# State-space groups of two batches with partitions of their own, and layer 1's experts from the first tick past layer 0's pieces

## The chip, the cores and the metric

The kernel runs on one core of one Trainium2 chip. The metric is the device time of one execution in microseconds (us): the median of several runs. The engines are called PE (TensorE; PEld is its weight load), DVE (VectorE), ACT (ScalarE), POOL (GpSimd) and SP (SyncE, which here issues DMAs). Each has an in-order queue of its own: an instruction that waits holds up all that stand behind it on its engine.

## What is computed

The input is x of shape 8 batches x 512 positions x 128 channels in float32. Two blocks follow one another; each normalises, applies a per-batch scale and shift, runs a mixer, and does the same again with a feed-forward part. Cut to what matters here:

```python
# layer 0: attention (16 heads of 8), then a mixture of 8 experts, the two best for each token, and a shared one
x = x + ga * attention(layernorm(x) * (1 + ca) + sa)
x = x + gb * moe(layernorm(x) * (1 + cb) + sb)
# layer 1: selective state space with 16 states
xc = depthwise_conv(h, conv_w) + conv_b            # along the 512 positions, 4 taps
delta, B_in, C = parts of (xc @ Win + b_in)        # 16 states each
dA = softplus(delta) * A;  A_bar = exp(dA)
B_bar = where(|A| < eps, 1 + dA/2 + dA*dA/6, (A_bar - 1) / A_safe) * B_in
h_t = A_bar_t * h_(t-1) + B_bar_t                  # a scan along the positions
x = x + ga * ((C * h) @ Wout + b_out)
# layer 1: feed-forward
x1 = h + silu(pointwise(depthwise_conv(h)))        # 3 taps
rw = softmax of the two best of (x1 @ router)      # weights of 8 experts
m = out_w @ sum over e of rw[e] * silu(expert_w[e] @ x1 + expert_b[e]) + out_b
x = x + gb * (r + ff(r)),  r = rmsnorm(x1 + m)
```

All 8 experts of layer 1 are computed for every token and weighted; the state-space scan treats each batch and state as one row.

## The kernel before, in words

The program has three stretches. The first, attention, is written out slot by slot and isn't touched. The second works off layer 0's experts: a list `work` of n = 62 pieces of 256 rows, 31 + 15 of them routed ones (they fetch rows and weights by DMA) and 12 + 4 that apply the shared expert. One pass of the loop at the end of the kernel is a **tick**: in tick i, PE turns the input of piece i + 2 (`pxt`, copied by DVE to `xt`), does the first layer of piece i (`ph`, with ACT's activation to `hid`) and the second layer of piece i - 1 (`pyb`, copied by ACT to `yb` or `sh`). After that come the steps of layer 1 that were set for this tick by hand: `when(t, do, ...)` appends a step to tick t, and steps of one tick come in the order in which they were set. From tick n = 62 on there are no pieces left, and a tick is only its steps. So ticks are an order, not a clock: each engine runs through its own queue as its waits allow.

Per batch the steps of layer 1 are, in this order:

- `gather` (POOL, eight indirect DMAs of `yg` per batch), `combine` (DVE: adds the two routed experts to `sh`, then to x), `two_stats`, `ssm_root`, `ssm_centre` (ACT makes `xh`), `ssm_channels` (PE turns it, `ptn`; ACT makes `hq`), `ssm_conv` (DVE makes `xc`, in two halves), `ssm_bias`.
- `ssm_project` (L1225): PE multiplies two batches' `xc` to `pj`, and ACT copies it to three tiles `dl`, `bi`, `ci`, whose rows are (batch, state): 32 rows for two batches.
- The **chain**, once per group of batches, on those tiles: `chain_1` (two operations on DVE, then Exp and Ln on ACT), `chain_2` (DVE, four operations on POOL to `da` and `ts`, then Exp on ACT to `ab`), `chain_3` (DVE: `bs`, in the buffer of `da`), `chain_4` (the scan to `u`, then `ci`). ACT's table has to be loaded anew when its function changes between the experts' GELU or SiLU and Exp or Ln. `out_weights` makes `wo` on POOL.
- The **lead-in** of a batch (`lead_in`): `ssm_out` (PE `py`, DVE adds to x), statistics, `ffn_centre`, `ffn_channels`, `ffn_pointwise` (L1327: PE `pw`; DVE and ACT make `sl`; POOL adds it to x1), `ffn_logits` (PE `pl`), `ffn_ranks` (two comparisons on DVE, and `rk_eq` on POOL), `ffn_chosen`, `ffn_tanh`, `ffn_gates`, `ffn_gates_out` (PE `pgt`, ACT `gt`, SP writes `g_rows`). `later(t, us)` turns a delay in us into ticks, at 4.0 us for a tick before n and 2.2 after.
- The **experts**: `expert_in` (PE `pe`, ACT `ye`), three ticks later `expert_gate` (DVE: t = ye * gb, and POOL adds the t of several experts), `expert_sum` (PE `r`). `ffn_spread` brings `gb` from `g_rows` by DMA, 512 KB each, with 5 buffers. `base[b]` is the tick of a batch's first expert: n + 5 + 8b, and 5 more for batches 6 and 7. Then `rms_*` and `ff_*`.

Before, the groups are (0,1,2,3), (4,5), (6,7), and all use the same rows, from 0 on, of single-buffered tiles. Group 0 is projected at ticks 44 and 49, its chain runs in ticks 50 to 54, its lead-ins start at ticks 55 to 58. The tile `sl` shares the two buffers of the tag `xc` with the convolution's output. The memory of the experts' tiles (`gb`, `t`, `ye`) is that of layer 0's weights and activations, so it is only taken at tick n.

Of the kernel before, what the change touches and what calls it, by code (L numbers as in the profile page):

```python
# [19 lines left out]
P = 128  # L20
# [48 lines left out]
def tile_adaln_two_blocks(  # L69
# [222 lines left out]
    with tc.tile_pool(name="at", bufs=2) as at, tc.tile_pool(name="sc", bufs=4, space=PSUM) as psc, tc.tile_pool(  # L292
# [597 lines left out]
        def when(t, do, *args):  # L890
            events.setdefault(t, []).append(lambda: do(*args))
# [296 lines left out]

        GROUPS = ((0, 1, 2, 3), (4, 5), (6, 7))

        def place_in_group(b):

            h = next(h for h, g in enumerate(GROUPS) if b in g)
            j = GROUPS[h].index(b)
            return h, slice(32 * (j // 2), 32 * (j // 2) + 32), j % 2


        def ssm_root(b):
# [25 lines left out]

        def ssm_project(h, s):  # L1225

            if s == 0:
                for name in ("dl", "bi", "ci"):
                    held[name] = lt([P, S], name)[0 : 16 * len(GROUPS[h]), :]
            ps = flat(bank("pj"))  # L1230
            for i in range(2):
                xc = held.pop(("xc", GROUPS[h][2 * s + i]))
                for k in range(3):
                    pin(
                        T.matmul(
                            ps[32 * k : 32 * k + 32, :],
                            lhsT=k1["wip"][:, k, i, :],
                            rhs=xc,
                            start=(i == 0),
                            stop=(i == 1),  # L1240
                        )
                    )
            for k, name in enumerate(("dl", "bi", "ci")):
                A.copy(held[name][32 * s : 32 * s + 32, :], ps[32 * k : 32 * k + 32, :])

        def chained(h, name, tag=None):
            held[name] = lt([P, S], name, tag=tag)[0 : 16 * len(GROUPS[h]), :]
            return held[name]

        def of_states(h, name, i=0):  # L1250
            return k1[name][0 : 16 * len(GROUPS[h]), i : i + 1]

        def chain_1(h, step):

            dl = held["dl"]
            if step == 0:
                V.tensor_scalar(dl, dl, of_states(h, "bias"), None, ALU.add)
                u = chained(h, "u")
                V.scalar_tensor_tensor(u, dl, -1.0, dl, ALU.mult, ALU.min)
            else:  # L1260
                u = held["u"]
                A.activation(u, u, AF.Exp)
                A.activation(u, u, AF.Ln, bias=ones[0 : 16 * len(GROUPS[h]), 0:1])

        def chain_2(h, step):
            dl, u = held["dl"], held["u"]
            if step == 0:
                V.scalar_tensor_tensor(dl, dl, 0.0, u, ALU.max, ALU.add)
                da = chained(h, "da")
                G.tensor_scalar(da, dl, of_states(h, "asm"), None, ALU.mult)  # L1270
                ts = chained(h, "ts")
                G.tensor_scalar(ts, da, 1.0 / 6.0, 0.5, ALU.mult, ALU.add)
                G.tensor_tensor(ts, ts, da, ALU.mult)
                G.tensor_scalar(ts, ts, 1.0, of_states(h, "small"), ALU.add, ALU.mult)
            else:
                A.activation(chained(h, "ab"), dl, AF.Exp, scale=of_states(h, "an"))

        def chain_3(h, step):
            if step == 0:
                bs = chained(h, "bs", "da")  # L1280
                V.tensor_scalar(bs, held["ab"], -1.0, of_states(h, "inva"), ALU.add, ALU.mult)
            else:
                bs = held["bs"]
                V.tensor_add(bs, bs, held["ts"])
                V.scalar_tensor_tensor(bs, held["bi"], of_states(h, "bias", 1), bs, ALU.add, ALU.mult)

        def chain_4(h):
            hh, ci = held["u"], held["ci"]
            V.tensor_tensor_scan(hh, held["ab"], held["bs"], 0.0, ALU.mult, ALU.add)
            V.scalar_tensor_tensor(ci, ci, of_states(h, "bias", 2), hh, ALU.add, ALU.mult)  # L1290
# [8 lines left out]
        def ssm_out(b):  # L1299

            _, r, _ = place_in_group(b)
            wo = held.pop(("wo", b))
            py = bank("py1")
            for c in range(NC4):
                pin(
                    T.matmul(
                        py[:, c, :], lhsT=held["ci"][r, c * P : (c + 1) * P], rhs=wo[r, :], start=True, stop=True
                    )
                )
            V.tensor_add(xs[b], xs[b], py)  # L1310
# [16 lines left out]
        def ffn_pointwise(b):  # L1327
# [4 lines left out]
            x1 = flat(lt([P, NC4, D], "x1", tag="sh", bufs=B))  # L1332
            sl = lt([P, S], "sl", tag="xc", bufs=2)
            if b in GROUPS[0]:

                th = lt([P, S], "th", tag="gt1", bufs=2)
                A.activation(th, pw, AF.Tanh, bias=k1["pwb2"], scale=0.5)
                V.tensor_scalar(sl, pw, k1["pwb"], 0.5, ALU.add, ALU.mult)
                V.scalar_tensor_tensor(sl, th, 1.0, sl, ALU.add, ALU.mult)
            else:  # L1340
                A.activation(sl, pw, AF.Silu, bias=k1["pwb"])
            G.tensor_tensor(x1, hq[:, 2 : S + 2], sl, ALU.add)
            x1s[b] = x1
# [224 lines left out]

        base = [n + 5 + NE * b + (5 if b > 5 else 0) for b in range(B)]
        for b in range(B):  # L1570
# [3 lines left out]
        for b in range(B):  # L1574
# [3 lines left out]
            for i in range(NE // 2):  # L1578
                when(max(t - 3 + 2 * i, n + 5), ffn_spread, b, i)
            when(t - 1, ffn_residual, b)  # L1580
            when(t + 5, ffn_bias, b)
# [20 lines left out]
        for b, ts in enumerate(  # L1602
# [4 lines left out]
                (43, 44, 45, 46, 47, 48, 50),  # L1607
                (46, 47, 48, 49, 50, 51, 52),
                (49, 50, 51, 52, 53, 54, 55),
            )  # L1610
# [9 lines left out]
            for i in range(2):  # L1620
                when(ts[5], ssm_conv, b, i)
            when(ts[6], ssm_bias, b)
        when(44, ssm_project, 0, 0)
        when(49, ssm_project, 0, 1)
        when(53, out_weights, 0)
        chain(0, 50, (0, 0, 1, 2, 3, 3, 4))
        for b in GROUPS[0]:
            lead_in(b, 55 + b)
        when(59, ssm_project, 1, 0)


# [134 lines left out]
```

## Time and profile before

| | us |
|---|---|
| median of 3 runs | 1101.12 (1100.58 to 1102.52) |
| the profiled execution's own time | 1077.77 |
| its span, first to last instruction | 1075.8 |
| mean granted PE clock in it | 0.968 |
| PE, DVE, ACT, POOL busy | 1017.4, 671.2, 640.2, 485.7 |
| last matmul of layer 0's pieces ends | 854.7 |
| first `ye` of layer 1's experts starts | 865.9 |
| first t = ye * gb starts | 878.4 |

In the rows of the profile a group reads: start, duration (or busy time and mean), engine, line, operation, output <- inputs, shape, count, and in brackets how long the engine stood idle before it and what ended that. L65 is the helper that records nearly all operations of DVE, ACT and POOL, so these are told apart by their tiles. A matmul in float32 makes two records. The last quarter of the span, from about 740 us, is where layer 1's steps lie; tick 44 starts at 748.8, tick 54 at 802.3, tick 60 at 836.2, by the rows of `ph`.

### The profile page before, as it was taken

To read this page: it belongs to the slowest core of one execution; us is meant where nothing else is said; L and a number is where in the kernel's file an instruction comes from. 1 tells how busy PE (TensorE), PEld (TensorE's weight loads), DVE (VectorE), ACT (ScalarE), POOL (GpSimd) and SP (SyncE) were. 2 spreads that over 40 slices of the span, in tenths; PEclk is the share of its full clock that TensorE was granted. 3 is DMA by queue.
4 is the path that set the end of the run, shared out by engine and by line. 5 is a ranking of instruction groups with operands and counts; after the bars stand their busy time and mean duration, and the time that the engine had idled before them with its cause. 6 is when DMAs were issued, how large, how long until landed. Compare 5 with 4: busy or idle time off the path is not lost.

```text
span 1075.8 us, 24284 instructions
## 1 busy us (share of the span) xinstructions
PE 1017.4 (95%) x9584; PEld 667.6 (62%) x9584; DVE 671.2 (62%) x1292; ACT 640.2 (60%) x1404; POOL 485.7 (45%) x763
## 2 busy tenths in 40 slices
PE   9999999999999999999999999999899957777988
PEld 8655555555555555555568899988788634444556
DVE  5567767687777768776822014236765469778663
ACT  1166667676666767766664555645585563575554
POOL 3301314264454726443464313278541484567661
PEclk9599999999999999999999999999999988898999
DMA  9970000000000000000025878723542042213051
GB/s 274 283 237 2 2 2 12 2 18 15 9 24 2 28 5 14 19 6 27 12 90 167 240 235 246 212 72 83 160 143 74 16 134 93 75 60 132 17 186 40
DMA packets 94129, 93.25 MB, mean 87 GB/s; under 512 B 7568, under 2 KB 72432, under 8 KB 94016
## 3 DMA queue, kind: packets, MB, share of 16 engines
q1 hardware_dynamic: 89744, 83.02, 25.7%
q0 software_dynamic: 4096, 8.40, 2.7%
q8 instruction: 75, 1.23, 0.5%
q10 hardware_dynamic: 176, 0.30, 0.1%
q14 instruction: 38, 0.31, 0.1%
HBM read 60.33 MB, written 31.35 MB: 85 GB/s over the span
## 4 chain that ended last, share of the span: by engine, by line
PE 79%; DVE 9%; POOL 4%; ACT 4%; issue 3%; DMA 1%; SPq 0%; DVEq 0%; POOLq 0%; ACTq 0%
PE ps L512 23%; PE av L533 12%; PE pyb L1023 9%; PE ph L1012 8%; PE pm L484 5%; PE pmt L500 2%; PE ppt L551 2%; PE pw L1331 2%; PE idle L416 2%; PE r L1420 1%; DVE t L65 1%; PE pqk L443 1%; PE prow L392 1%; DVE xc L65 1%; PE pe L1432 1%
## 5 line engine op out<-in xcount | busy, mean ns | idle before, releaser
L65 DVE TENSOR_REDUCE mpad<-pm 128x2 f32<-128x1024 f32 x256 | 310.6, 1219 | 126.8 <-PE pm L484 126.4
L65 ACT ACTIVATE es<-ps 128x512 f32<-128x512 f32 x512 | 275.3, 598 | 141.5 <-PE pm L484 117.1
L512 PE MATMUL ps<-qt,kt 32*128 32x512 f32 x1024 | 291.4, 630 | 1.4 <-ACT es L65 0.7
L484 PE MATMUL pm<-kt,qt 32*128 32x512 f32 x1024 | 279.8, 646 | 0.3 <-DVE mpad L65 0.3
L533 PEld LDWEIGHTS av<-es,vaug 128*32 128x32 f32 x4096 | 104.2, 110 | 94.0 <-ACT part L65 43.2
L533 PE MATMUL av<-es,vaug 128*32 128x128 f32 x4096 | 137.7, 276 | 0.0
L512 PEld LDWEIGHTS ps<-qt,kt 32*128 32x128 f32 x1024 | 94.3, 183 | 63.2 <-issue 30.9
L65 ACT ACTIVATE hid<-ph,bias 128x256 f32<-128x256 f32 x184 | 72.1, 476 | 58.7 <-PE ph L1012 58.5
L767 POOL DMA_INDIRECT x_rows<-tok,ux x64 | 65.1, 1018 | 70.4 <-DMA x_rows<-tok,ux 61.5
L1023 PEld LDWEIGHTS pyb<-w2b,hid 128*128 128x128 f32 x736 | 90.9, 194 | 5.1 <-ACT hid L65 2.4
L1023 PE MATMUL pyb<-w2b,hid 128*128 128x128 f32 x736 | 91.4, 278 | 2.0 <-ACT hid L65 2.0
L1012 PE MATMUL ph<-xt,w1b 128*128 128x256 f32 x368 | 89.0, 386 | 0.0
L484 PEld LDWEIGHTS pm<-kt,qt 32*128 32x128 f32 x1024 | 78.2, 186 | 10.9 <-ACT kf L65 5.4
L65 POOL TENSOR_SCALAR qt<-qf,mask,zero 128x512 f32<-128x512 f32 x31 | 24.0, 776 | 130.2 <-PE pm L484 103.3
L1043 POOL DMA_INDIRECT yg<-y_rows,yrows x64 | 64.6, 1010 | 36.4 <-issue 18.2
L1432 PE MATMUL pe<-x,l1w_sb 128*128 128x512 f32 x128 | 71.9, 676 | 5.1 <-ACT ye L65 5.1
L1012 PEld LDWEIGHTS ph<-xt,w1b 128*128 128x128 f32 x368 | 67.7, 194 | 7.5
L65 DVE COPY xt<-pxt 128x256 f32<-128x256 f32 x46 | 19.1, 419 | 77.2 <-PE pxt L937 77.2
L65 ACT ACTIVATE ye<-pe,pc 128x512 f32<-128x512 f32 x64 | 43.2, 683 | 38.5 <-PE pe L1432 31.7
L65 POOL TENSOR_TENSOR t<-t 128x512 f32<-128x512 f32 x34 | 47.8, 1408 | 22.9 <-DVE t L65 21.4
L65 DVE TENSOR_TENSOR t<-ye,gb 128x512 f32<-128x512 f32 x64 | 54.5, 874 | 2.3 <-POOL t L65 2.3
L1420 PE MATMUL r<-l1w_sb,t 128*128 128x128 f32 x240 | 35.6, 297 | 16.4 <-POOL t L65 13.0
(301 smaller groups left out, 1562.5 us busy)
## 6 DMA issues: line engine op xcount, KB each, us to landing
x_rows<-zeros SPq DMA_DIRECT2D x16, 1024.0 KB
gb<-g_rows SPq DMA_DIRECT2D x32, 512.0 KB
w1b<-in_w1t SPq DMA_DIRECT2D x46, 256.0 KB
w2b<-in_w2t SPq DMA_DIRECT2D x46, 256.0 KB
xg<-x_rows SPq DMA_DIRECT2D x46, 128.0 KB
y_rows<-yb SPq DMA_DIRECT2D x46, 128.0 KB
x<-in_x SPq DMA_DIRECT2D x8, 256.0 KB
h_chan<-hf SPq DMA_DIRECT2D x8, 256.0 KB
```

Source lines behind the costliest of these rows:

```text
L65: return lambda *args, **kwargs: self.pin(call(*args, **kwargs))
L416: pin(T.matmul(ps[:, 0, :], lhsT=ident, rhs=ident, start=True, stop=True))
L484: T.matmul(pm[:, i, :], lhsT=qt[r : r + 32, qc * P : (qc + 1) * P], rhs=kt[r : r + 32, :], start=True, stop=True,)
L500: pin(T.transpose(pt[:, c, :], mpads[g % 4][:, c, :], ident))
L512: T.matmul(ps, lhsT=kt[r : r + 32, kc * P : (kc + 1) * P], rhs=qt[r : r + 32, :], start=True, stop=True)
L533: T.matmul(ps[32 * j : 32 * j + 32, 0, :], lhsT=vaugs[b % 2][:, kc, 4 * j + m, :], rhs=es_of[4 * g + kc, j][:, q], start=(kc == 0), stop=( ...
L767: nc.gpsimd.indirect_dma_start(out=x_rows[h], out_offset=IndirectOffsetOnAxis(ap=chosen["ux", b][:, k, c : c + 1], axis=0), in_=half[h]["t ...
L1012: pin(T.matmul(ph[:, f, :], lhsT=it["w1"][:, f * P : (f + 1) * P], rhs=it["x"], start=True, stop=True))
L1023: T.matmul(py[:, c, :], lhsT=it["hid"][:, f, c * P : (c + 1) * P], rhs=it["w2"][:, f, :], start=(f == 0 and "shared" not in it), stop=(f = ...
L1043: nc.gpsimd.indirect_dma_start(out=gathered[b][:, k, c, :], out_offset=None, in_=y_rows[h], in_offset=IndirectOffsetOnAxis(ap=half[h]["yro ...
L1420: T.matmul(ffn[b]["r"][:, c, :], lhsT=x[:, c * P : (c + 1) * P], rhs=w, start=(start and c == 0), stop=stop, skip_group_check=True,)
L1432: pin(T.matmul(pe, lhsT=l1w_sb[:, 2 + e, :], rhs=x1s[b], start=True, stop=True))
```

## The change

What it does:

- The groups are (0,1), (2,3), (4,5), (6,7). Group h has rows 32h to 32h + 31 of seven tiles (`dl`, `bi`, `ci`, `u`, `da`, `ts`, `ab`) that are allocated once; `bs` is written over `da`. So there are four chains of 32 rows instead of one of 64 and two of 32.
- Group 0 is projected at tick 44, with its chain in ticks 45 to 49 and lead-ins at 50 and 51; group 1 at tick 50, chain in 51 to 55, lead-ins at 56 and 57. Group 2 is projected at tick 60 (59 before).
- For batches above 1 the two halves of `ssm_conv` are in two ticks. Batches 4 and 5 are combined at ticks 50 and 53 (46 and 49 before), and their later steps follow.
- The experts start at tick n instead of n + 5. Nearly all that follows is 5 ticks sooner; the chain of group 2 and the lead-ins of batches 4 and 5 are 4 ticks sooner. The gathers of batches 6 and 7 keep ticks n - 2 to n + 3.
- `ffn_pointwise` writes into x1 at once; the tile `sl` is gone.

```diff
-        GROUPS = ((0, 1, 2, 3), (4, 5), (6, 7))
+        GROUPS = ((0, 1), (2, 3), (4, 5), (6, 7))
...
+            return b // 2, rows_of(b // 2), b % 2
+
+        def rows_of(h):
+            return slice(32 * h, 32 * h + 32)
...
+        def ssm_project(h):
+
+            if h == 0:
+                for name in ("dl", "bi", "ci", "u", "da", "ts", "ab"):
+                    k1[name] = lt([P, S], name)
             ps = flat(bank("pj"))
...
-                A.copy(held[name][32 * s : 32 * s + 32, :], ps[32 * k : 32 * k + 32, :])
+                A.copy(of(h, name), ps[32 * k : 32 * k + 32, :])
+
+        def of(h, name):
+            return k1[name][rows_of(h), :]
...
         def chain_3(h, step):
+            bs = of(h, "da")
             if step == 0:
-                bs = chained(h, "bs", "da")
-                V.tensor_scalar(bs, held["ab"], -1.0, of_states(h, "inva"), ALU.add, ALU.mult)
+                V.tensor_scalar(bs, of(h, "ab"), -1.0, of_states(h, "inva"), ALU.add, ALU.mult)
...
-            sl = lt([P, S], "sl", tag="xc", bufs=2)
-            if b in GROUPS[0]:
+            if b < 4:
 
                 th = lt([P, S], "th", tag="gt1", bufs=2)
                 A.activation(th, pw, AF.Tanh, bias=k1["pwb2"], scale=0.5)
-                V.tensor_scalar(sl, pw, k1["pwb"], 0.5, ALU.add, ALU.mult)
-                V.scalar_tensor_tensor(sl, th, 1.0, sl, ALU.add, ALU.mult)
+                V.tensor_scalar(x1, pw, k1["pwb"], 0.5, ALU.add, ALU.mult)
+                V.scalar_tensor_tensor(x1, th, 1.0, x1, ALU.add, ALU.mult)
             else:
-                A.activation(sl, pw, AF.Silu, bias=k1["pwb"])
-            G.tensor_tensor(x1, hq[:, 2 : S + 2], sl, ALU.add)
+                A.activation(x1, pw, AF.Silu, bias=k1["pwb"])
+            G.tensor_tensor(x1, hq[:, 2 : S + 2], x1, ALU.add)
...
-        base = [n + 5 + NE * b + (5 if b > 5 else 0) for b in range(B)]
+        base = [n + NE * b + (5 if b > 5 else 0) for b in range(B)]
...
-                when(max(t - 3 + 2 * i, n + 5), ffn_spread, b, i)
-            when(t - 1, ffn_residual, b)
+                when(max(t - 3 + 2 * i, n), ffn_spread, b, i)
+            when(max(t - 1, n), ffn_residual, b)
...
-                (46, 47, 48, 49, 50, 51, 52),
-                (49, 50, 51, 52, 53, 54, 55),
+                (50, 51, 52, 53, 54, 55, 57),
+                (53, 54, 55, 56, 57, 58, 60),
...
-                when(ts[5], ssm_conv, b, i)
+                when(ts[5] + (i if b > 1 else 0), ssm_conv, b, i)
...
-        when(44, ssm_project, 0, 0)
-        when(49, ssm_project, 0, 1)
-        when(53, out_weights, 0)
-        chain(0, 50, (0, 0, 1, 2, 3, 3, 4))
-        for b in GROUPS[0]:
-            lead_in(b, 55 + b)
-        when(59, ssm_project, 1, 0)
+        for h, t, lags in ((0, 44, (0, 1, 1, 2, 3, 4, 4)), (1, 50, (0, 0, 1, 2, 3, 3, 4))):
+            when(t, ssm_project, h)
+            when(t + 2, out_weights, h)
+            chain(h, t + 1, lags)
+            for b in GROUPS[h]:
+                lead_in(b, t + 6 + b % 2)
+        when(60, ssm_project, 2)
...
-        when(n + 8, out_weights, 1)
-        chain(1, n + 5, (0, 1, 2, 4, 6, 7, 8))
-        lead_in(4, n + 14)
-        lead_in(5, n + 18)
-        for b, t in ((6, n + 10), (7, n + 13)):
+        when(n + 3, out_weights, 2)
+        chain(2, n + 1, (0, 1, 2, 4, 6, 7, 8))
+        lead_in(4, n + 10)
+        lead_in(5, n + 14)
+        for b, t in ((6, n + 5), (7, n + 8)):
...
-        when(n + 20, out_weights, 2)
-        when(n + 27, ssm_project, 2, 0)
-        chain(2, n + 28, (0, 1, 2, 4, 6, 7, 8))
-        lead_in(6, n + 37)
-        lead_in(7, n + 44)
+        when(n + 15, out_weights, 3)
+        when(n + 22, ssm_project, 3)
+        chain(3, n + 23, (0, 1, 2, 4, 6, 7, 8))
+        lead_in(6, n + 32)
+        lead_in(7, n + 39)
```

More of the change, by code (lines that the diff above doesn't have):

```diff
@@ L1186, in channels @@
             return hq
-        GROUPS = ((0, 1, 2, 3), (4, 5), (6, 7))
+        GROUPS = ((0, 1), (2, 3), (4, 5), (6, 7))
         def place_in_group(b):
-            h = next(h for h, g in enumerate(GROUPS) if b in g)
-            j = GROUPS[h].index(b)
-            return h, slice(32 * (j // 2), 32 * (j // 2) + 32), j % 2
+            return b // 2, rows_of(b // 2), b % 2
+        def rows_of(h):
+            return slice(32 * h, 32 * h + 32)
         def ssm_root(b):
@@ L1223, in ssm_conv @@
                 held.pop(("hp", b))
[L1225 to L1229, printed above, removed]
+        def ssm_project(h):
+            if h == 0:
+                for name in ("dl", "bi", "ci", "u", "da", "ts", "ab"):
+                    k1[name] = lt([P, S], name)
             ps = flat(bank("pj"))
-            for i in range(2):
-                xc = held.pop(("xc", GROUPS[h][2 * s + i]))
+            for i, b in enumerate(GROUPS[h]):
+                xc = held.pop(("xc", b))
                 for k in range(3):
@@ L1243, in ssm_project @@
             for k, name in enumerate(("dl", "bi", "ci")):
-                A.copy(held[name][32 * s : 32 * s + 32, :], ps[32 * k : 32 * k + 32, :])
-        def chained(h, name, tag=None):
-            held[name] = lt([P, S], name, tag=tag)[0 : 16 * len(GROUPS[h]), :]
-            return held[name]
+                A.copy(of(h, name), ps[32 * k : 32 * k + 32, :])
+        def of(h, name):
+            return k1[name][rows_of(h), :]
         def of_states(h, name, i=0):
-            return k1[name][0 : 16 * len(GROUPS[h]), i : i + 1]
+            return k1[name][rows_of(h), i : i + 1]
         def chain_1(h, step):
-            dl = held["dl"]
+            dl, u = of(h, "dl"), of(h, "u")
             if step == 0:
                 V.tensor_scalar(dl, dl, of_states(h, "bias"), None, ALU.add)
-                u = chained(h, "u")
                 V.scalar_tensor_tensor(u, dl, -1.0, dl, ALU.mult, ALU.min)
             else:
-                u = held["u"]
                 A.activation(u, u, AF.Exp)
-                A.activation(u, u, AF.Ln, bias=ones[0 : 16 * len(GROUPS[h]), 0:1])
+                A.activation(u, u, AF.Ln, bias=ones[rows_of(h), 0:1])
         def chain_2(h, step):
-            dl, u = held["dl"], held["u"]
+            dl, u, da, ts = (of(h, name) for name in ("dl", "u", "da", "ts"))
             if step == 0:
                 V.scalar_tensor_tensor(dl, dl, 0.0, u, ALU.max, ALU.add)
-                da = chained(h, "da")
                 G.tensor_scalar(da, dl, of_states(h, "asm"), None, ALU.mult)
-                ts = chained(h, "ts")
                 G.tensor_scalar(ts, da, 1.0 / 6.0, 0.5, ALU.mult, ALU.add)
@@ L1275, in chain_2 @@
             else:
-                A.activation(chained(h, "ab"), dl, AF.Exp, scale=of_states(h, "an"))
+                A.activation(of(h, "ab"), dl, AF.Exp, scale=of_states(h, "an"))
         def chain_3(h, step):
+            bs = of(h, "da")
             if step == 0:
-                bs = chained(h, "bs", "da")
-                V.tensor_scalar(bs, held["ab"], -1.0, of_states(h, "inva"), ALU.add, ALU.mult)
-            else:
-                bs = held["bs"]
-                V.tensor_add(bs, bs, held["ts"])
-                V.scalar_tensor_tensor(bs, held["bi"], of_states(h, "bias", 1), bs, ALU.add, ALU.mult)
+                V.tensor_scalar(bs, of(h, "ab"), -1.0, of_states(h, "inva"), ALU.add, ALU.mult)
+            else:
+                V.tensor_add(bs, bs, of(h, "ts"))
+                V.scalar_tensor_tensor(bs, of(h, "bi"), of_states(h, "bias", 1), bs, ALU.add, ALU.mult)
         def chain_4(h):
-            hh, ci = held["u"], held["ci"]
-            V.tensor_tensor_scan(hh, held["ab"], held["bs"], 0.0, ALU.mult, ALU.add)
+            ci, hh = of(h, "ci"), of(h, "u")
+            V.tensor_tensor_scan(hh, of(h, "ab"), of(h, "da"), 0.0, ALU.mult, ALU.add)
             V.scalar_tensor_tensor(ci, ci, of_states(h, "bias", 2), hh, ALU.add, ALU.mult)
@@ L1306, in ssm_out @@
                     T.matmul(
-                        py[:, c, :], lhsT=held["ci"][r, c * P : (c + 1) * P], rhs=wo[r, :], start=True, stop=True
+                        py[:, c, :], lhsT=k1["ci"][r, c * P : (c + 1) * P], rhs=wo[r, :], start=True, stop=True
                     )
```

## The prediction

> **What bounds the kernel now.** I read the summary page first, then busy time by stretch, then the timelines of the engines around the seam between layer 0's expert pieces (ticks 0 to 62) and layer 1's experts (tick 62 on).
>
> ```profile
> PE 1017.4 (95%) x9584; PEld 667.6 (62%) x9584; DVE 671.2 (62%) x1292; ACT 640.2 (60%) x1404; POOL 485.7 (45%) x763
> ...
> PE   9999999999999999999999999999899957777988
> ```
> ```profile
> 748.80:808.00 59.20, 53.66 (x339) 46.25 (x338) 44.82 (x111) 41.62 (x90) 29.51 (x42) 0.94 0.52 150
> 808.00:854.70 46.70, 45.91 (x288) 36.00 (x287) 22.89 (x75) 25.96 (x61) 10.68 (x14) 1.00 0.17 47
> 854.70:878.40 23.70, 14.10 (x53) 7.01 (x51) 12.21 (x39) 10.99 (x17) 17.14 (x19) 0.86 0.41 127
> 878.40:925.00 46.60, 34.47 (x131) 19.83 (x131) 41.59 (x97) 24.91 (x51) 28.35 (x29) 0.89 0.28 91
> ```
>
> Columns: stretch, length, busy time of PE, PEld, DVE, ACT, POOL, then granted clock. Up to 854.7 TensorE is the bound (45.91 of 46.70). Then nothing is full for 23.7 us: the last piece is done at 854.7 and the first gated expert comes at 878.44. Behind it VectorE is nearly full (41.59 of 46.60). The seam is what the change works on. POOL, then DVE there:
>
> ```profile
> 867.22 0.94 POOL L1043 DMA_INDIRECT yg<-y_rows,yrows  x1 [0.30 <-issue]
> ...
> 875.61 0.73 POOL L65 TENSOR_TENSOR rk_eq<-rk_eq,tri 128x256 f32<-128x256 f32 x1
> 878.63 1.92 POOL L65 TENSOR_SCALAR da<-dl,asm 32x512 f32<-32x512 f32 x1 [2.29 <-DVE dl L65]
> ...
> 885.06 1.25 POOL L65 TENSOR_TENSOR t<-t 128x512 f32<-128x512 f32 x1
> ```
> ```profile
> 870.19 0.42 DVE L65 TENSOR_TENSOR rk_gt<-rk_gt,rk_eq 128x256 f32<-128x256 f32 x1 [5.85 <-POOL rk_eq L65]
> ...
> 878.44 0.67 DVE L65 TENSOR_TENSOR t<-ye,gb 128x512 f32<-128x512 f32 x1
> ...
> 883.63 4.19 DVE L65 TENSOR_SCALAR bs<-ab,inva 32x512 f32<-32x512 f32 x1
> ```
>
> VectorE waits 5.85 us for an rk_eq that stands in POOL's queue behind gathers, one each 1.25 us. So POOL's queue, with the rankings, sets the seam. The bs row is a state-chain step that took 4.19 us while POOL was busy beside it (1.58 in the chain before, at 801.62).
>
> Two more places:
>
> ```profile
> 769.43 1.48 PE L1184 MATMUL ptn<-ident,xh 128*128 128x128 f32 x4 [3.33 <-ACT xh L65]
> ...
> 770.97 3.42 PE L1012 MATMUL ph<-xt,w1b 128*128 128x256 f32 x8
> ...
> 793.94 3.60 PE L1023 MATMUL pyb<-w2b,hid 128*128 128x128 f32 x16 [2.04 <-ACT hid L65]
> 799.84 1.95 PE L1023 MATMUL pyb<-w2b,hid 128*128 128x128 f32 x16
> ```
> ```profile
> 788.14 1.28 ACT L65 ACT_TABLE_LOAD   x1
> 789.44 0.63 ACT L65 ACTIVATE u<-u 64x512 f32<-64x512 f32 x1
> ...
> 944.14 0.69 ACT L65 ACTIVATE sl<-pw,pwb 128x512 f32<-128x512 f32 x1 [4.87 <-PE pj L1235]
> ```
>
> **The change part by part.** Spans below are of the profiled execution: 1075.8 us between instructions, 1077.77 in all. The median of the runs shown is 1101.12, 23.35 more, which no row explains; I take gains off it unscaled.
>
> *One more chain in the pieces.* Groups of two batches make four chains, not three, and two stand before tick 62, not one. On ScalarE the program gains five table loads: 5 x 1.28 = 6.4, plus Exp, Ln, Exp at 0.63 + 0.72 + 0.72: 8.5 us. VectorE gains eight operations (0.45 + 0.68 + 0.67 + 1.58 + 0.68 + 0.74 + 1.21 + 0.74 = 6.8), POOL four (1.56 + 0.62 + 1.26 + 0.69 = 4.1). Half the partitions don't make them cheaper: bs, ts and ci have rows of the same length at 32 and at 64 partitions. VectorE has 14 of 59 us free there and hides it, POOL 30. ScalarE hides only part: its queue is in order, hid stands behind the loads, and TensorE waits for hid. The chain of before cost TensorE 2.04 waiting, 1.65 in the slow pyb (3.60 against 1.95) and some 0.6 in the two groups behind: 4.3. Two rules of the Trainium skill bear on this. ScalarE: Activation LUTs (What ACT_TABLE_LOAD costs) adds a drain of about 1.38 us to each load; the row has the next activation 0.02 us after the 1.28 load, so I take 6.4, where the rule would make 13.3, nearly 7 us more in front of hid and most of the gain gone. TensorE: Matmul & The Clock Gate (HAM oscillation) has the clock fall only after gaps above some 3.4 us; here gaps of 2.04 and 3.33 were both followed by slow matmuls. By the rule a chain costs 2.0, by the rows 4.3; I take 4.3.
>
> *The convolution split over two ticks.* At 763.39 the three longer convolution steps (4.79 us) kept xh of the next batch back: 3.33 waiting and about 2.6 in slow matmuls (ptn 1.48 against 0.60, ph 3.42 against 1.89, pyb 0.2). Now only the first half stands ahead of xh, so this 5.9 mostly goes; the first chain's Exp and Ln fall into the same tick and eat some of it.
>
> *Lead-ins sooner.* Rankings, tanh, gates and gates out of batches 0 and 1 move into the pieces, also batch 3's pointwise. Ahead of the gathers' place in tick 60 TensorE gets one pw (2.7), two pl (1.9), two pgt (1.2), a ptn (0.6), less a pj (1.9): +4.5, paid in full, since it is full there. Stalls between 748.8 and 854.7 were 6.2 waiting and 4.9 slow: 11.1. After: two chains at 4.3, less overlap with the old convolution stall, about 7.5 (bounds 4 and 15). So tick 60 comes 4.5 + 7.5 - 11.1 = 0.9 later (-3 to +8).
>
> *The seam.* Five ticks without experts go; all later work keeps its order, except that chain 2 and the lead-ins of 4 and 5 come one tick later beside the experts. The 16 gathers do not move: ticks 60 to 65, now with experts beside them and POOL's first t sum behind them. POOL from the first gather (847.28) to the end of the chain's ts (884.26) took 37.0. Now: 16 x 1.25 = 20, one x (1.1), two rk_eq (1.5), wo (0.85), four chain operations (5.35) = 28.8, and about 2.4 waiting for batch 3's pointwise: 31.2. That is 5.8 sooner, less 0.9. VectorE in turn waits at bs for POOL's ts (they share the da tile), and behind bs all gates are queued; but a combine pair (1.73) and a gate (0.68) that stood behind bs now stand ahead of it: +2.4. VectorE is the bound from there, so this carries on. Seam: 5.8 - 0.9 + 2.4 = 7.3. The spreads (SP, 0.33 each, 512 KB) are issued ticks sooner; SP is idle from 826 to 864, and their data wait for g_rows alone: nothing.
>
> *No sl tile.* sl shared two buffers with the convolution: at 944.14 ScalarE had waited 4.87 for a projection that comes later, with POOL's x and a t sum queued behind. Now the pointwise writes x1 itself. VectorE idled 2.26 and TensorE 1.75 after it: I take 2.7 (0 to 4.9).
>
> Sum: 7.3 + 2.7 = 10.0; 1101.1 - 10.0 = 1091.1, of the profiled kind 1067.8.
>
> **Rivals.**
> - *The whole seam goes.* If POOL's sums can lag (t has five buffers, and POOL idled 18 us between 885 and 925), the first gate sets the pace: about 8 us behind the pieces' end at some 856, 864 against 878.4: 14.4, plus 2.7: 17, 1084. For it: VectorE's own queue is short in ticks 62 to 65. Against: bs.
> - *The gathers swallow it.* POOL without a gap starves bs longer, tick 60 is 4 late, sl's wait was covered: 5.8 - 4 + 1 = 3, 1098. For it: the 4.19. That the row groups of one tile bind each other, so that the chains don't run free, would cost about as much.
> - *Slower: ScalarE in ticks 46 to 53.* Two chains, four xh and two projections' copies share that queue with hid. If three bursts each stall TensorE as xh did (5.9) and the convolution's stall stays, 23.6 replaces 11.1: tick 60 is 17 late, and 5.8 + 2.4 + 2.7 - 17 = -6: 1107. It decides once tick 60 is more than 10.9 late, that is with stalls over 17.5. For it: ScalarE is at 41.62 of 59.20 already. Against: the second pair of loads (799.5 to 802.8) stalled TensorE nowhere.
>
> **How the numbers follow.** Likeliest case (1086 to 1096) 0.46; whole seam (below 1086) 0.15; swallowed (1096 to 1101) 0.21; slower 0.18. Within 0.2% (2.2 us, about what a measurement of this kernel can tell from no change) are 1098.9 to 1103.3: part of the third case and a little of the last, 0.10; slower beyond 0.16; faster 0.74. The range leaves out the fastest tenth and the slowest tenth: 1083 to 1105.
>
> **What would show it.** Right: no xh stall of ptn at tick 47 to 48, pyb waiting twice for hid behind table loads, the first gather within 847 to 852, POOL's first t sum at 876 to 883 of the span, no wait of batch 5's pointwise for pj, the span near 1066. Wrong: TensorE idle over 10 us or a granted clock below 0.92 in ticks 44 to 60; the first t sum after 885; pxt copies late because VectorE is full in ticks 50 to 57.

## The result and the profile after

Side by side, the changed kernel took 1112.77 us (median of 4 runs, 1110.32 to 1118.78) and the kernel before 1100.85 (4 runs, 1099.77 to 1102.52): a ratio of 1.0115, 95% interval 1.0073 to 1.0157. It is slower by 1.15%; forecast was 1091.1. In that comparison both kernels carried some 23 us that no later comparison shows (last section), so the two are read below from a second comparison: 1088.11 beside 1078.16, ratio 1.0110 (1.0056 to 1.0165).

The summary page of the first profile of the changed kernel (own time 1110.32, span 1108.5), which answers to the one of before:

```profile
PE 1023.9 (92%) x9584; PEld 670.8 (61%) x9584; DVE 667.7 (60%) x1300; ACT 648.4 (58%) x1412; POOL 491.6 (44%) x767
...
PE   9999999999999999999999999869888965777988
```

TensorE does the same 9584 matmuls in 6.5 us more busy time. Its row has three slices of 8 on the way to the seam (the 6 and 5), where before had one; the 86 left of them, from 693 to 748 us, holds the 23 us, ahead of all that was changed.

The stretches of the second profile (own time 1086.70, span 1084.7), cut at the same events as before: tick 44; the point 1.8 us into tick 55; the end of the last piece; the first gated expert; then on to 925. Columns: stretch, length, busy time of PE, PEld, DVE, ACT, POOL, then granted clock.

```profile
749.90:823.90 74.00, 61.24 (x359) 49.61 (x358) 49.87 (x133) 52.71 (x104) 33.58 (x45) 0.92 0.44 125
823.90:871.70 47.80, 47.19 (x288) 36.60 (x287) 28.88 (x78) 24.76 (x60) 15.83 (x21) 0.99 0.31 95
871.70:879.60 7.90, 7.90 (x33) 4.56 (x32) 4.35 (x14) 7.01 (x9) 6.66 (x7) 1.00 0.13 34
879.60:925.00 45.40, 21.93 (x99) 14.07 (x98) 32.83 (x77) 17.49 (x32) 29.29 (x27) 0.74 0.25 79
```

The first stretch grew from 59.20 to 74.00, and TensorE, which was busy for all but 5.5 us of it, is now idle for 12.8 and at a granted clock of 0.92 (0.94 before). The second is as full as it was. The empty seam of 23.70 is now 7.90. But behind it TensorE does 21.93 in 45.40 where it did 34.47 in 46.60: the first experts come early and then stand still.

What TensorE waited for from 748 to 862, the view of waits, changed kernel; then the same of a repeat of the kernel before (span 1076.4). Columns: waiting line, releaser, total, times, longest.

```profile
PE pyb L1023 <- ACT hid L65: 6.5, 3, 3.5
PE py L1300 <- DVE ci L65: 3.4, 2, 2.9
PE pxt L937 <- ACT yb L65: 2.3, 1, 2.3
```
```profile
PE ptn L1184 <- ACT xh L65: 3.4, 1, 3.4
PE pyb L1023 <- ACT hid L65: 2.0, 1, 2.0
PE py L1306 <- DVE ci L65: 0.8, 1, 0.8
```

The wait for xh is gone, as meant. In its place hid is waited for three times (once before), yb once, and the wait for ci has grown from 0.8 to 3.4.

Profiled executions stand up to 8 us apart at tick 44 already (744.9 to 752.8), which the change does not reach. So I compare lengths from tick 44 on, by the rows of ph and pyb, one profiled execution each. The two of before differ by 0.9 in ticks 44 to 60, the two of the change by 1.7; a difference of 2 us or less between two rows shows little by itself.

| kernel | 44 to 50 | 50 to 55 | 55 to 60 | 44 to 60 | last piece's end to first t sum | last piece's end to the end |
|---|---|---|---|---|---|---|
| before, repeat | 34.2 | 23.9 | 30.3 | 88.3 | 30.3 | 221.4 |
| changed, repeat | 32.9 | 39.3 | 30.1 | 102.3 | 27.7 | 213.1 |
| before_conv_split | 32.8 | 23.1 | 29.4 | 85.3 | 30.3 | 220.9 |
| before_no_sl | 33.3 | 23.9 | 30.2 | 87.4 | 30.3 | 220.9 |
| before_gathers_last | 34.5 | 23.5 | 30.0 | 88.1 | 24.9 | 217.9 |
| before_no_tables | 35.1 | 19.5 | 30.7 | 85.3 | 30.3 | 218.5 |
| before_split_gathers_last | 33.3 | 22.3 | 29.4 | 85.0 | 24.1 | 217.0 |
| after_experts_late | 33.0 | 40.6 | 29.2 | 102.8 | 28.9 | 215.9 |
| after_gathers_last | 32.9 | 40.4 | 31.0 | 104.3 | 17.0 | 209.9 |
| after_no_tables | 26.9 | 39.8 | 29.2 | 95.9 | 27.9 | 213.3 |
| after_edges_on_dve | 31.4 | 37.5 | 29.9 | 98.8 | 27.8 | 213.1 |
| after_edges_no_tables | 25.5 | 37.9 | 29.1 | 92.5 | 27.8 | 213.0 |
| after_edges_lead_2_no_tables | 26.3 | 27.2 | 36.2 | 89.7 | 28.0 | 213.3 |
| after_edges_lead_1 | 34.1 | 29.9 | 33.1 | 97.1 | 27.3 | 213.4 |
| after_edges_lead_1_gathers_last | 32.3 | 29.3 | 35.2 | 96.9 | 16.1 | 206.7 |

The change loses 14.0 us between ticks 44 and 60, 1.0 more up to the last piece's end, and has 8.3 back by the end: 6.7 from tick 44 on, at the lower end of the 6 to 18 that the interval of the ratio gives. The loss lies in ticks 50 to 55.

### The profile page after: what moved, and what is told of

Its sections match the earlier page's. It is cut to its first block, busy times and chain, and to the rows that moved or that the text cites. A ratio compares the mean times of both kernels' runs of the same rounds, so it can differ in the third digit from the quotient of the medians.

```text
span 1108.5 us, 24293 instructions
## 1 busy us (share of the span) xinstructions
PE 1023.9 (92%) x9584; PEld 670.8 (61%) x9584; DVE 667.7 (60%) x1300; ACT 648.4 (58%) x1412; POOL 491.6 (44%) x767
## 4 chain that ended last, share of the span: by engine, by line
PE 74%; DVE 10%; POOL 6%; issue 5%; ACT 4%; DMA 1%; SPq 0%; POOLq 0%; DVEq 0%; ACTq 0%
PE ps L512 21%; PE av L533 11%; PE pyb L1023 8%; PE ph L1012 8%; PE pm L484 5%; PE pmt L500 2%; PE pw L1325 2%; PE ppt L551 2%; DVE t L65 1%; PE prow L392 1%; PE idle L416 1%; PE pqk L443 1%; PE r L1413 1%; DVE xc L65 1%; POOL yg L1043 1%
## 5 line engine op out<-in xcount | busy, mean ns | idle before, releaser
L1413 PE MATMUL r<-l1w_sb,t 128*128 128x128 f32 x240 | 35.2, 295 | 35.9 <-POOL t L65 33.6
L1425 PE MATMUL pe<-x,l1w_sb 128*128 128x512 f32 x128 | 66.8, 638 | 0.6 <-ACT ye L65 0.6
L1413 PEld LDWEIGHTS r<-l1w_sb,t 128*128 128x128 f32 x240 | 32.1, 205 | 46.3 <-POOL t L65 39.2
L65 ACT ACTIVATE ye<-pe,pc 128x512 f32<-128x512 f32 x64 | 43.1, 684 | 28.9 <-PE pe L1425 25.3
```

Source lines behind the costliest of these rows:

```text
L65: return lambda *args, **kwargs: self.pin(call(*args, **kwargs))
L1413: T.matmul(ffn[b]["r"][:, c, :], lhsT=x[:, c * P : (c + 1) * P], rhs=w, start=(start and c == 0), stop=stop, skip_group_check=True,)
L1425: pin(T.matmul(pe, lhsT=l1w_sb[:, 2 + e, :], rhs=x1s[b], start=True, stop=True))
```

## The experiments

Theory after the result: the pieces are late because of ScalarE's table loads for two chains. Rivals: the first chain's own way is too long for its ticks; the seam is what failed.

**Both kernels again.** No edit. First the kernel before:

> The kernel before, unchanged, for a second profile. In the profile of the changed kernel TensorE crawls from 711 to 737 us, one instruction each 2 us with no wait that the profile shows, and loses 22 us in a stretch that the change does not touch; the first profile of before has no such crawl, and its own execution (1077.77) lies 23 us under its median (1100.85). Theory: the crawl belongs to nearly every execution of both kernels and was missing in that one profile; then this execution takes 1098 to 1103 us, and its trace shows TensorE waiting 18 to 24 us between 700 and 745. Rival: the crawl is the changed kernel's own; then no crawl here, and if the time is near 1100 the 23 us lie elsewhere, spread over the span.

Measured 1078.24, with TensorE at full pace where the slow passage was expected: that theory fell, and the extra 23 us left the comparison. The next run's profile has no slow passage either, so they are not the changed kernel's own. Then the change:

> The changed kernel once more, beside the same runs of before as the others. The runs so far had before at 1077.3 us (no crawl of TensorE), and the kernel with the changed pieces but experts five ticks later at 1088.8. Theory: the five ticks bring little, since the first sum waits for the gathers either way: 1087 to 1091, a ratio to before of 1.009 to 1.013, as in the first comparison. Rival: the five ticks bring 8 to 10 us as the two profiles' tails suggest, and the 1.0115 came from the crawl: 1078 to 1081.

Measured 1088.11 beside 1078.16, ratio 1.0110. The loss is the change's own and has nothing to do with the 23 us.

**The convolution's halves in two ticks, alone.**

```diff
-                when(ts[5], ssm_conv, b, i)
+                when(ts[5] + (i if b > 1 else 0), ssm_conv, b, i)
```

> Before with one part of the change: the two halves of the convolution of batches 2 to 5 stand in two ticks. Theory: the wait of TensorE for xh at tick 48 (3.33 us, with 2.6 us of slow matmuls behind it) goes, and the rest stays: 4 to 6 us less than before, near 1096. Rival: the second half only moves into the next tick, where it delays the copies of the pieces' inputs, so that the stall moves along: within 1.5 us of before.

Measured 1074.69 (11 runs) beside 1077.26, ratio 0.9973 (0.9949 to 0.9996), 3.0 us in the stretch. This is less than the 4 to 6 that were expected: ptn still waits for xh, 2.42 us instead of 3.41. The trace shows what took the convolution's place: at 765.72 a step of 128x4 on VectorE, on the way to xh, takes 3.21 us while POOL works beside it; the same step took 0.16 in the kernel before.

**No sl tile, alone** (the last hunk of the change's `ffn_pointwise`, on the kernel before).

> Before with one part of the change: the pointwise writes x1 itself, and the tile sl, which shares two buffers with the convolution, is gone. Theory: ScalarE's wait of 4.87 us at batch 5's pointwise goes, and VectorE and GpSimd behind it gain 2 to 3 us: 1097.5 to 1099. Rival: TensorE had other work in those 5 us and VectorE is the bound there, so nothing is gained: within 1 us of 1100.9.

Measured 1078.98 (20 runs), ratio 1.0008 (0.9992 to 1.0023). ScalarE's 4.87 us wait is gone (the pointwise's activation waits 1.18), and the time does not move: that wait was covered.

**The change with its experts five ticks later again** (`base`, spreads, residual, chains 2 and 3 and lead-ins 4 to 7 shifted back).

> The changed kernel with its experts, and all that follows them, 5 ticks later again as in the kernel before; the four chains, the early lead-ins and the x1 without sl stay. Theory: the change loses about 15 us between ticks 44 and 61 and gets back 8 to 10 by the five ticks; then this kernel keeps the loss without the gain: 5 to 9 us above the changed one, 1118 to 1122. Rival: the five ticks bring nothing, since the first sum on GpSimd stands behind the same gathers either way (TensorE waits 20.4 us for it in the changed kernel): within 3 us of the changed kernel's 1112.8.

Measured 1088.76 (4 runs), ratio 1.0095 (1.0062 to 1.0128). The five ticks bring 2.8 us of the trace behind the pieces (215.9 to 213.1) and nothing that the runs can tell.

**Batch 7's gathers behind the first experts**, on each kernel:

```diff
-            when(n - 2 + k // 3, gather, PB[0] + k // 8, k % 8)
+            when(n - 2 + k // 3 if k < 8 else n + 4 + (k - 8) // 2, gather, PB[0] + k // 8, k % 8)
```

> The changed kernel with batch 7's eight gathers moved behind the first sums on GpSimd: two in each of ticks 66 to 69, not in ticks 62 to 65. Its combine at ticks 70 to 73 still finds them landed. Theory: GpSimd's queue of gathers sets the first sum (923.6 us in the changed kernel's profile, with TensorE idle 20.4 us before it): the sum comes 8 to 10 us sooner, and the kernel is 5 to 9 us faster than the changed one. Rival: VectorE's own queue with the chain's steps sets the pace of the experts: under 2 us.

> The kernel before with batch 7's gathers moved in the same way, to ticks 71 to 74 (two each). Theory: in the kernel before, too, the rankings and the first sum stand behind the gathers (VectorE waited 5.85 us for one): 3 to 6 us less than before, near 1073. Rival: the chain from logits to gates and spread sets the seam there: within 1.5 us of before.

On the change 1086.82, ratio 1.0107 (1.0051 to 1.0163): the first t sum comes 10.7 us nearer to the last piece, the end 3.2, and the runs show under 2. On before (n + 9) 1074.34, ratio 0.9980 (0.9964 to 0.9995). So the gathers hold the first sum, and the late pieces are a loss of their own.

**No table loads in the first two chains.** GELU takes the place of Exp, Ln and Exp there; the state space of batches 0 to 3 is not computed.

```diff
-                A.activation(u, u, AF.Exp)
-                A.activation(u, u, AF.Ln, bias=ones[rows_of(h), 0:1])
+                exp, ln = (AF.Exp, AF.Ln) if h > 1 else (AF.Gelu_apprx_tanh, AF.Gelu_apprx_tanh)
+                A.activation(u, u, exp)
+                A.activation(u, u, ln, bias=ones[rows_of(h), 0:1])
...
-                A.activation(of(h, "ab"), dl, AF.Exp, scale=of_states(h, "an"))
+                A.activation(of(h, "ab"), dl, AF.Exp if h > 1 else AF.Gelu_apprx_tanh, scale=of_states(h, "an"))
```

> The changed kernel with Exp, Ln and Exp in the chains of the first two groups replaced by the GELU that the pieces use, so that ten table loads of 1.28 us in ticks 44 to 55 go; this leaves out the true softplus and decay of batches 0 to 3. Theory: ScalarE's bursts of loads are the larger part of the loss in the pieces, two waits for hid of 2.27 and 2.45 with some 2.3 of slow matmuls behind each: 8 to 11 us faster than the changed kernel. Rival: the loss is VectorE's in ticks 49 to 57 and the moved work: under 4 us.

Measured 1079.29 (20 runs), ratio 1.0005 (0.9988 to 1.0023): 8.8 us faster than the change, 6.4 in the stretch. All waits for hid are gone, and the one for yb is 0.7 instead of 2.3. But one wait is longer:

```profile
788.83 2.04 PE L1301 MATMUL py<-wo,ci 32*128 32x128 f32 x8 [7.08 <-DVE ci L65]
790.80 3.63 PE L1235 MATMUL pj<-xc,wip 128*32 128x512 f32 x12
```

TensorE reached tick 50 sooner, and then waited 7.08 us instead of 2.92 for the first chain's last result, ci. Behind it pj took 3.63 us; it takes 1.92 in the kernel before. So a second delay lay beside the first. VectorE, then POOL, then TensorE of the change, repeat, show where it comes from:

```profile
779.71 3.98 DVE L65 TENSOR_SCALAR xc<-hq,pc 128x511 f32<-128x511 f32 x1 [4.13 <-POOL hq L65]
...
784.40 0.47 DVE L65 TENSOR_SCALAR da<-ab,inva 32x512 f32<-32x512 f32 x1
...
788.11 1.21 DVE L65 TENSOR_TENSOR_SCAN u<-ab,da 32x512 f32<-32x512 f32 x1
789.36 0.74 DVE L65 SCALAR_TENSOR_TENSOR ci<-ci,sbias,u 32x512 f32<-32x512 f32 x1
```
```profile
773.34 2.24 POOL L65 TENSOR_SCALAR da<-dl,asm 32x512 f32<-32x512 f32 x1 [5.33 <-DVE dl L65]
...
778.38 1.25 POOL L65 TENSOR_TENSOR x<-x,gab_rows 128x512 f32<-128x512 f32 x1
779.59 0.12 POOL L65 MEMSET hq<- 128x1 f32 x2
```
```profile
790.24 1.47 PE L1300 MATMUL py<-wo,ci 32*128 32x128 f32 x8 [2.92 <-DVE ci L65]
791.64 3.20 PE L1235 MATMUL pj<-xc,wip 128*32 128x512 f32 x12
```

Read it backwards. py waits for ci; ci stands on VectorE behind a convolution that waited 4.13 us; what it waited for is 0.12 us of POOL, the zeros at the edges of hq, and these stand in POOL's queue behind the first chain's four operations and an addition to x. Then the convolution took 3.98 us beside POOL's additions (0.54 when POOL was idle, in the kernel before). From here on the theory was that the zeros are the second delay.

**The edge columns written by VectorE**, alone and with the tables away:

```diff
-                G.memset(hq[:, 0:lead], 0.0)
+                (V if lead == 1 and b < 6 else G).memset(hq[:, 0:lead], 0.0)
```

(and the same for the tail's column.)

> The changed kernel with one thing moved: the zeros at the edge columns of hq (two columns of one element a row) are written by VectorE and not by POOL, for the convolution's hq of batches 0 to 5. In the trace of the changed kernel VectorE stands 4.13 us before the convolution of batch 3, for these two columns, which stand in POOL's queue behind the four operations of the first chain; the convolution then takes 3.98 us instead of 0.6 beside POOL's additions to x, and the first chain's scan stands behind it, and TensorE's py waits 2.92 us for that. Theory (a short POOL write on the way of the first chain is part of the loss): that wait of py goes, and the kernel is 3 to 5 us faster than the changed one: 1083 to 1085 beside a before of 1077 to 1078, a ratio near 1.006. Rival (only ScalarE's table loads bind): within 1.5 us of the changed kernel, ratio near 1.010.

> The kernel above, and besides the chains of the first two groups use GELU in place of Exp, Ln and Exp, so that ScalarE loads no table there; what is computed is no longer the state space of batches 0 to 3. With the tables alone away TensorE waited 7.08 us for the first chain's ci (2.92 with them), so the two delays lie beside each other. Theory (two delays of about equal length, tables and the chain's way through POOL and VectorE, either of which holds tick 50): with both away the kernel is 5 to 7 us faster than with the tables alone away (1079.3), so 1072 to 1074, a ratio near 0.995, and tick 60 comes no later than in the kernel before plus the 4.5 us of moved matmuls. Rival (what is left is simply TensorE's and VectorE's added work): within 2 us of 1079.

Alone 1084.93 (6 runs) beside 1076.19, ratio 1.0077 (1.0052 to 1.0102); 3.5 us in the stretch. That is the theory's number, but its interval overlaps that of the change, and the wait that was to go is there: py waits 2.85 us. With the tables away 1077.27 (14 runs), ratio 1.0001 (0.9983 to 1.0019): the rival's number. The trace has 3.4 us less in the stretch, of which the runs show next to nothing, and py still waits 5.91.

Why the wait stays, VectorE and then POOL show, edges alone:

```profile
773.63 1.53 DVE L65 TENSOR_SCALAR xc<-hq,pc 128x511 f32<-128x511 f32 x1 [0.79 <-ACT hq L65]
775.20 6.03 DVE L65 SCALAR_TENSOR_TENSOR xc<-hq,pc,xc 128x511 f32<-128x511 f32 x1
```
```profile
775.69 2.49 POOL L65 TENSOR_TENSOR x<-x,gab_rows 128x512 f32<-128x512 f32 x2
778.18 2.49 POOL L65 TENSOR_TENSOR x<-x,gab_rows 128x512 f32<-128x512 f32 x2
```

The convolution no longer waits 4.13 us for the zeros, but its next step takes 6.03 us and ends just after POOL's four additions to x; in the change, where it came behind them, that step took 0.75. With the tables away two such steps took 6.57. From dl to the end of ci the first chain needs 17.0 us with the edges on VectorE and 17.6 in the change. So the zeros alone did not hold it: once they are away, by the rows, the convolution beside POOL's additions does. Of the 3.5 us some 1.4 come sooner, at batch 2's convolution, whose zeros had stood behind gathers in POOL's queue (VectorE waited 3.13 us for them), and 1.6 because py and pj took 1.12 and 1.92 us this time. Moving the additions to another place was not tried, so that the wait for ci is theirs is argued and not shown.

**One chain's tables in the kernel before** (the same edit there; batches 0 to 3 again).

> The kernel before with GELU in place of Exp, Ln and Exp in the one chain that stands in layer 0's pieces; what is computed is no longer the state space of batches 0 to 3. It prices one chain's table loads in the old place. Theory (one chain's loads cost TensorE 4.3 us, as the prediction had it from a 2.04 wait and a slow group behind it): 1074, ratio 0.996; then the loads of two chains would be worth 8.6, which is what the changed kernel lost. Rival (in the old place the loads are mostly hidden, and it is the new place, beside the convolutions and projections of batches 2 and 3, that makes them dear): within 1.5 us of before.

Measured 1076.69 (14 runs), ratio 0.9997 (0.9981 to 1.0012). In the trace ticks 50 to 55 lose 4.4 us and the stretch 3.0; in the runs nothing. The profiled execution was 2.6 us late by tick 30 already, where nothing was edited. Behind the last piece it has 2.9 us less than before, where nothing was edited either. So single profiles differ by as much as this edit is worth in them.

**More ticks for the first chain.** Lead-ins of batches 0 and 1 later, by two ticks without tables, by one with them:

```diff
-                lead_in(b, t + 6 + b % 2)
+                lead_in(b, t + 6 + b % 2 + (2 if h == 0 else 0))
```

> The changed kernel with hq's edge columns written by VectorE, GELU in place of Exp, Ln and Exp in the chains of the first two groups (their state space is left out), and the lead-ins of batches 0 and 1 two ticks later (52 and 53), so that the first chain has seven ticks instead of five. With the same lead-ins as in the change this kernel took 1077.3, and TensorE waited 5.91 us for ci with slow matmuls behind it (pj 3.63 instead of 1.9, py 2.04 instead of 1.1), 8.7 in all. Theory (that one wait is the rest of the loss): the last piece ends 7 to 9 us sooner, near 856 of the span, and the kernel takes 1070 to 1072, a ratio near 0.994. Rival (TensorE's moved matmuls are the rest, and the wait only shows where slack lay): within 2 us of 1077, and TensorE idles elsewhere in ticks 50 to 58.

> The changed kernel with hq's edge columns written by VectorE, and the lead-ins of batches 0 and 1 one tick later (51 and 52); all is computed, and all tables are loaded. With the edges alone it took 1084.9, and py waited 2.85 us for ci. Theory (the first chain is too long for five ticks): that wait goes, with its slow matmuls 4 us: 1081, a ratio near 1.004. Rival (the tick that is freed is filled by hid behind the second chain's tables, which moves with nothing): within 1.5 us of 1084.9.

Without tables 1074.46 (22 runs) beside 1077.64, ratio 0.9972 (0.9953 to 0.9991), about 3 us better than without the two ticks; 2.8 in the stretch. That is between the two expectations. TensorE's waits there:

```profile
PE ptn L1184 <- ACT xh L65: 2.3, 1, 2.3
PE pj L1235 <- DVE xc L65: 1.5, 1, 1.5
```

The wait for ci is gone, but two others stand in its place. With the tables 1081.57 (11 runs), ratio 1.0043 (1.0019 to 1.0067): 0.34% better than with the edges alone, near the 4 us expected, of which the stretch shows 1.7. The wait for ci is gone here too, but the waits for hid rose from 6.2 to 8.4 us, which is the rival's mechanism at a smaller size.

**All three mended**: edges, one tick, and batch 7's gathers last.

> The kernel above, and batch 7's gathers in ticks 66 to 69 instead of 62 to 65, behind the first experts' sums on POOL. Theory (once the pieces are on time the seam is POOL's, and its first sum sets the rest): 3 to 5 us under the kernel above, 1077, about even with the kernel before. Rival (VectorE behind the first gate is the bound, as in the changed kernel, where the same move gave under 2): within 2 us of the kernel above.

Measured 1075.57 (22 runs) beside 1077.64, ratio 0.9973 (0.9959 to 0.9988). This has all of the change in it and beats the kernel before. Here the gathers' move is worth 6.7 us of the trace and 0.7% of the time, in the trace twice what it gave either other kernel; why, is not settled.

**The two small gains on the kernel before.**

> The kernel before with the two small gains joined: the convolution's halves of batches 2 to 5 in two ticks (alone ratio 0.9973), and batch 7's gathers in ticks 71 to 74 (alone 0.998). Theory (the first shortens the pieces, the second the seam, so they add): ratio 0.9953, 1072 to 1073. Rival (both end in the same first gate, where VectorE is the bound behind): no better than the convolution alone, 0.997 to 0.998.

Measured 1074.06 (22 runs) beside 1076.19, ratio 0.9980 (0.9966 to 0.9995): no better than either alone, though the trace of one execution adds them up (span 1070.0). Its interval overlaps that of the mended change; the runs do not tell which is the best.

## Why the prediction was wrong

**The step that failed: "stalls 11.1, after about 7.5, so tick 60 comes 0.9 later (−3 to +8)".** Tick 60 came 14.0 later, because the stalls did not fall to 7.5 but rose to some 21.7. Counted in the rows of ticks 44 to 60 as the prediction counted them, waiting and slow matmuls together:

| TensorE's stalls, us | before, repeat | change, repeat | in the prediction, after |
|---|---|---|---|
| behind ScalarE's chain work: hid, in the change yb too | 4.3 | 14.1 | 8.6 for two chains |
| for ci | 0.8 | 5.0 | absent |
| for xh | 5.9 | 0 | part of −1.1, with the rest |
| the rest | 0.5 | 2.6 | |
| sum | 11.5 | 21.7 | 7.5 |

The other part of the 14.0 is moved matmuls: 3.9, the foreseen 4.5 less a pgt that stands behind tick 60's ph.

The experiments took parts away one after the other. Each step but the last changes one thing, the first in both kernels; the runs are differences of medians or of ratios:

| step | us of ticks 44 to 60 | us in the runs | in the prediction |
|---|---|---|---|
| the change's tables (102.3 − 95.9), less those of before (88.3 − 85.3) | 3.4 | 8.8 less 0.3 | 4.3 for one more chain |
| edge columns off POOL's queue (95.9 − 92.5) | 3.4 | 0.4; with tables 3.6 | absent |
| two more ticks for the first chain (92.5 − 89.7) | 2.8 | 3.1 | absent |
| what is left against before without tables (89.7 − 85.3) | 4.4 | | −3.4: moved matmuls 4.5, the convolution −5.9, overlap and other stalls −2.0 |
| sum | 14.0 | | 0.9 |

The two tables answer different questions. The first says what TensorE waited for; the second says what came back when that was taken away. With the tables away nearly all of the 14.1 went, but the stalls for ci grew from 5.0 to 11.1 (7.5 of it waiting), so the trace gives back only 6.4. For the price of one more chain the traces say 3.4 and the runs some 8, and this stays open. By the runs the loss goes when the two chains' tables go (ratio 1.0110 with them, 1.0005 without), but with all tables loaded the edges and one more tick take more than half of it away too (1.0043). The parts overlap and do not add.

The slower rival, "decides with stalls over 17.5", put the stalls at 23.6, tick 60 at 17 late and the time at 1107. Its direction, its place and its cause, bursts on ScalarE that hold hid, were right by the rows: three such bursts of 6.0, 4.1 and 4.1 us are the 14.1. The convolution's stall, which it kept, went, and the wait for ci, which it had not, came.

Point by point:

- *A chain's price.* 4.3 each, read from the one chain of before, was too small for the new place: by the rows the first cost 6.0 behind hid and the second 8.2 behind hid and yb. "The second pair of loads stalled TensorE nowhere" held in the kernel before; in the change the second pair of each chain did. ScalarE of the change, repeat, with the second chain's first loads and its second pair, then TensorE:

```profile
804.24 1.28 ACT L65 ACT_TABLE_LOAD   x1
805.54 0.72 ACT L65 ACTIVATE u<-u,ones 32x512 f32<-32x512 f32 x1
806.27 1.28 ACT L65 ACT_TABLE_LOAD   x1
807.57 1.57 ACT L65 ACTIVATE hid<-ph,bias 128x256 f32<-128x256 f32 x4
...
816.39 1.28 ACT L65 ACT_TABLE_LOAD   x1
817.68 0.72 ACT L65 ACTIVATE ab<-dl,an 32x512 f32<-32x512 f32 x1
818.41 1.28 ACT L65 ACT_TABLE_LOAD   x1
819.70 1.57 ACT L65 ACTIVATE hid<-ph,bias 128x256 f32<-128x256 f32 x4
821.14 0.39 ACT L65 COPY yb<-pyb 128x256 f32<-128x256 f32 x1
```
```profile
808.10 3.58 PE L1023 MATMUL pyb<-w2b,hid 128*128 128x128 f32 x16 [2.46 <-ACT hid L65]
...
821.59 0.69 PE L937 MATMUL pxt<-ident,xg 128*128 128x128 f32 x2 [2.29 <-ACT yb L65]
```
```profile
808.10:811.50 3.40, 3.40 (x16) 3.40 (x17) 3.29 (x7) 3.40 (x10) 3.14 (x3) 0.52 0.13 39
```

  Each load is followed 0.02 us later by its activation; no row has the 1.38 us drain that the Trainium skill gives in ScalarE: Activation LUTs (What ACT_TABLE_LOAD costs). And 2.46 us of idling were followed by a group of 3.58 us instead of 1.95, at a granted clock of 0.52 (last row), though the Trainium skill, TensorE: Matmul & The Clock Gate (HAM oscillation), names only gaps above some 3.4 us. So the rows were the better guide to both. But a gap of this length does not always cost it: in the kernel with the edges on VectorE a wait of 2.85 us was followed by matmuls at a clock of 1.00 (787 to 791 us).
- *"VectorE and POOL hide it."* This is where the wait for ci comes from. By share of busy time both had room. By order they had not: with five ticks from projection to lead-in, the first chain's scan stood on VectorE behind a convolution that waited for POOL and then ran slowly beside POOL's additions. The prediction had seen such a row at the seam (bs, 4.19 us "while POOL was busy beside it") and did not look for it in the pieces. It costed each engine's work and never laid out the chain's way from dl to ci against the tick in which py asks for it.
- *The convolution.* "This 5.9 mostly goes": it went in the change, where ptn no longer waits. Done alone it gave 3.0. As a stall it was replaced: the kernel with two more ticks still has about as much stalling, 9.3, as before without tables, 8.8.
- *Moved matmuls.* 4.5 foreseen, 3.9 by the rows up to tick 60.
- *The seam and sl.* 7.3 + 2.7 = 10.0 foreseen, 8.3 came, but not as told. POOL from the first gather to the end of the chain's ts took 36.0 (863.36 to 899.34, the changed kernel's repeat), where 31.2 was foreseen and before had 37.0:

```profile
863.36 1.10 POOL L1043 DMA_INDIRECT yg<-y_rows,yrows  x1 [0.16 <-issue]
...
871.48 1.09 POOL L65 TENSOR_TENSOR x<-hq,x 128x512 f32<-128x512 f32 x1 [3.24 <-DVE x L65]
...
893.70 0.86 POOL L65 TENSOR_TENSOR wo<-wop,ga_rows 32x128 f32<-32x128 f32 x2 [1.66 <-DMA yg<-y_rows,yrows]
...
898.37 0.97 POOL L65 TENSOR_SCALAR ts<-ts,small 32x512 f32<-32x512 f32 x1
899.41 1.26 POOL L65 TENSOR_TENSOR t<-t 128x512 f32<-128x512 f32 x1
```

  Waits of 3.24 for batch 3's pointwise, 1.58 and 1.66 stand where 2.4 had been allowed for, and TensorE's first r waits 20.38 us for the t sum. The gain comes later: the first sum is 2.6 nearer to the last piece's end, batch 3's first gate 9.9 (92.3 against 102.2). Most of it is not the five ticks': with the experts where they were, 5.5 of the 8.3 are there already. What is left for it are the steps that moved into the pieces and no longer stand among the first experts; that was not tried by itself.
- *No sl tile.* 2.7 taken from 0 to 4.9; alone it gave nothing in the runs, so the lower end was right.
- *Signs that were named.* Of those for being right, three came: no wait of ptn for xh at ticks 47 to 48, no wait of batch 5's pointwise for pj, pyb waiting for hid behind table loads (three times for the two named). Three did not: the first gather at 863.4 for 847 to 852, the first t sum at 899.4 for 876 to 883, the span at 1084.7 for 1066. Of those for being wrong, "TensorE idle over 10 us in ticks 44 to 60" (13.1) and "the first t sum after 885" came true; the granted clock stayed at 0.93 there (below 0.92 was named), and pxt was not held up by VectorE.

## What to carry to other kernels

Moving a chain of steps over several engines into a full stretch is costed by its length against the ticks it gets, from its first input to the instruction that asks for its last result, each engine's queue laid out in order; the busy shares say only that the work fits somewhere. Look also at what runs beside the moved steps: here VectorE's convolution took 6.03 us for a step of 0.75 while POOL added to x, so that taking away the 0.12 us of zeros ahead of it shortened the chain's way only from 17.6 to 17.0 us. After taking a cause away, read again whether the wait went, and not only whether the time fell. A chain's price read in one place need not hold in another: 4.3 us before, 6.0 and 8.2 here. An idle gap that a move closes is worth its length only if nothing in front of it grows, so cost the stretch that pays at least as carefully as the one that gains.

## What the runs showed of the hardware that was not expected

The 23 us of the first comparison: in the first profile of the change TensorE nearly stops at 713 us, in layer 0's shared pieces, ahead of all that was changed. Its timeline there:

```profile
717.33 0.90 PE L1012 MATMUL ph<-hl,ws 128*128 128x256 f32 x3 [1.84 <-issue]
720.14 1.44 PE L1012 MATMUL ph<-hl,ws 128*128 128x256 f32 x3 [1.91 <-issue]
...
727.88 0.37 PE L982 MATMUL pyb<-b_sb,gt 9*128 9x128 f32 x1 [1.73 <-issue]
```

One to three matmuls, then some 2 us of waiting for nothing that the profile shows, up to 733, while POOL issues a gather each 1.25 us. From 710 to 737 TensorE was busy 11.85 of 27.00 us; in the kernel before 27.00. The instruction queue moved two blocks between 690 and 740, in the kernel before three: instructions of TensorE that came late would fit, but no run shows whether that is the cause. In the later comparisons no profile shows it, and every run of the kernel before took 1066 to 1085 us.
